# Second attention: where POOL's operations stand, the outputs' division in two parts, two DVE sums in steps of their own

## The chip, the core and the metric

The kernel runs on one core of a Trainium2 chip. The metric is device time in microseconds (us), lower is better. The engines are named as the profile names them: PE is the matrix engine and PEld its weight loads, DVE the vector engine, ACT the scalar engine, POOL the general engine, SP the engine whose queue issues most of the DMAs. A wait belongs to the engine that waits; each engine runs its own instructions in a fixed order, and semaphores order them against the other engines.

## The reference

The input has 16 batches of 512 tokens with 128 features. Two layers follow each other. The first adds a four-fold stack of a state-space block, 16-head attention and a feed-forward block to a feed-forward with ternary weights. It ends before the stage that is changed. The second adds a local attention and a mixture of eight experts. The local attention, cut to what is computed:

```python
q = (x @ Wq) ... ; kv = (x @ Wkv) ...             # 16 heads of 64
q = rotary(q) * SCALE; kv = rotary(kv)
lkv = look_around(kv in windows of 128)           # the window before and its own
lkv = layernorm(lkv, ln_local_g, ln_local_b)      # over the 64 of a head
pkv = softmax(gkv @ Wproj, over each 16 tokens)   # a summary of each segment
gkv = layernorm(sum of gkv * pkv, ln_global_g, ln_global_b)
sim = [q . gkv (32 segments, masked), q . lkv (masked)]
attn = softmax(sim); out = (attn @ [gkv, lkv]) @ Wout + bout
```

The mixture sends each token to one expert (a softmax over eight scores, the largest taken, a rank within the expert, a limit on its places), computes two matmuls with a relu between, weights the result and adds it back at the token's row.

## The kernel before

The second attention works on **units**: 64 tiles of 128 tokens (`u`; four of them, `t` = 0 to 3, are the 512 tokens of a batch). A unit has four **groups** of four heads. Nothing reorders instructions afterwards: each engine runs them in the order in which the program below emits them.

**The main loop.** For group `i` it calls `scores(i)`, then `weights_by_key(i - 1, two)` and `values(i - 2, two)` for `two` = 0 and 1, and after each of these `work(1)`. A group therefore has six calls of `work`. `work` walks a list of generators, the *streams*, and lets each that is due run to its next `yield`. `yield -n` makes a stream due again n calls later; `yield n` does the same and also ends that call of `work`; `yield 0` leaves it due at the next call. If a unit's `front` is not finished when its scores are to begin, the loop calls `work` until it is.

**The streams.** `front(u)` makes the unit's queries and keys and is begun two units ahead. `back(u)` finishes a unit's output and is inserted first in the list when its last scores are done. `routing` computes the expert of each token, scatters the tokens' rows to the experts' places in HBM (`xe_d`, one indirect DMA from POOL's queue for each 128 tokens), and then runs 16 expert halves (`expert_half`). `results` gathers each tile's expert output (`gy`, an indirect DMA from POOL's queue, three buffers), loads the attention's result (`res`) and adds the two on DVE; it begins when the experts are done and can then take one tile after another until it has caught up with the tiles stored.

**One front, with the profile's names.** `xu` is loaded. Two matmuls `m_kv` give keys; DVE multiplies them with cosines (`by_cos`, L1192) and ACT copies them (`raw`, L1193). POOL multiplies `raw` with sines (L1196) and forms `kv` in two halves (L1199, L1200). Four times four matmuls `m_q` and four DVE products `q` (L1210) follow, and POOL adds them in pairs to `qt` (L1218). Then the layer norm over a head: DVE's sum `hm` (L1221) and difference `hd` (L1223), POOL's product `by_w` (L1227), ACT's square `hq` (L1229), DVE's sum `hv` (L1232), ACT's two steps and POOL's five for the root `hr` (L1236 to L1242), and DVE's sum `pl` of `by_w` (L1244). `pl` is transposed on PE (`m_plt`), DVE makes `n` (L1253), `smx` and `se`, and ACT the exponential. After `ss` POOL divides `se` (L1264). Eight transposes `m_nt` of `n` are copied by ACT to the keys `lkt` (L1272); POOL makes the values `lk` in two operations, a product (L1281) and a sum (L1309). `se` goes through `m_pwp` to the segment sums `m_gp`, whose norm (`gm`, `gd`, `gr`, with POOL's L1307 and L1308) gives the segments' values `gv` (L1313, L1314). These go to HBM and come back in four small transfers to `gvb` (L1333), and through `m_gkt` to the keys.

**Scores and values.** `s` is four matmuls; DVE adds the mask and takes the maximum (the pair `pr` and `am`, L1360); ACT takes the exponential and its sum (L1361) and copies the segments' part (`pg`). PE transposes the weights (`gp`, `pp_0`, `pp_1`, L1376 and L1383); DVE and ACT copy them (`gt`, `pt`). `values` adds the products in `o`, which ACT copies to `ot` (L1414), half a unit at a time. The scores are 288 wide, in the first unit of a batch 160.

**One back.** DVE's reciprocal of the sums (L1421), its transpose `m_rd`, a copy to HBM and two broadcasting loads `rb`; POOL multiplies `ot` with `rb` (L1440); nine matmuls `m_po`, DVE's `ro` (L1447) and a store to `r_d`.

**Buffers.** PSUM has five banks for `s`, `gp` and `pp` in turn, two for all that begins with `m_`, and one for `o`. A matmul that takes a bank waits for the reader of what was in it. Most of `front`'s large SBUF tiles have one buffer.

Of the kernel before, what the change touches and what calls it, by code (L numbers as in the profile page):

```python
# [14 lines left out]
ALU = mybir.AluOpType  # L15
# [54 lines left out]
def tile_kernel(  # L70
# [16 lines left out]
    nc = tc.nc  # L87
# [38 lines left out]
    with (  # L126
# [46 lines left out]
        def misc(name):  # L173
            return ps_m.tile([P, S], F32, name=f"m_{name}", tag="m")

        def mm(out, lhsT, rhs, first=True, last=True):
            nc.tensor.matmul(out, lhsT=lhsT, rhs=rhs, start=first, stop=last)  # L177
# [725 lines left out]
        while done_t[0] < n_cycles or ready or streams or due or deferred:  # L903
# [20 lines left out]
            if ready and ready[0][0] <= tick[0]:  # L924
                at, k, i = ready.pop(0)
# [3 lines left out]
            if do_t and done_t[0] % 4 == 3:  # L929
                k, t = divmod(done_t[0], 8)  # L930
# [14 lines left out]
    with (  # L945
# [12 lines left out]
        def const(name):  # L958
            at, n = CONST[name]
            return cst[:, at : at + n]  # L960
# [12 lines left out]
        def row(i):  # L973
            return rows_sb[:, i * DH1 : (i + 1) * DH1]
# [8 lines left out]
        heads = [P, H1, DH1]  # L983
# [155 lines left out]
        def results():  # L1139
# [3 lines left out]
            for t in range(NT):  # L1143
# [12 lines left out]
                nc.vector.scalar_tensor_tensor(res, gy, pk[:, t : t + 1], res, ALU.mult, ALU.add)  # L1156
                nc.sync.dma_start(out[t * P : (t + 1) * P, :], res)

        class Unit:
            pass  # L1160

# [5 lines left out]
        def front(u):  # L1167

            U = units[u] = Unit()
# [13 lines left out]
            def halves(v):  # L1183
                return v.rearrange("p h (a d) -> p h a d", a=2)

            raw = wk.tile(heads, F32, name=f"raw_{u}", tag="raw", bufs=1)
# [6 lines left out]
                nc.scalar.copy(raw[:, 8 * c : 8 * c + 8], psh)  # L1193
                yield 1
            sink = const("sink")[:, t * 32 : (t + 1) * 32].unsqueeze(1).unsqueeze(1).broadcast_to(pair)
            nc.gpsimd.tensor_tensor(halves(raw), halves(raw), sink, ALU.mult)  # L1196
            kv = wk.tile(heads, F32, name=f"kv_{u}", tag="kv", bufs=2)
            k, c_, s_ = halves(kv), halves(by_cos), halves(raw)
            nc.gpsimd.tensor_tensor(k[:, :, 0, :], c_[:, :, 0, :], s_[:, :, 1, :], ALU.subtract)  # L1199
            nc.gpsimd.tensor_tensor(k[:, :, 1, :], c_[:, :, 1, :], s_[:, :, 0, :], ALU.add)  # L1200
            U.qt = wk.tile([P, NHP, P], F32, name=f"qt_{u}", tag="qt", bufs=3)
            for c in range(2):
                parts = []
                for a, name in enumerate(("cosq", "sinq")):
                    ps = misc(f"q_{u}_{c}_{a}")
                    for i in range(4):
                        at = (4 * c + i) * P
                        mm(ps[:, i * P : (i + 1) * P], wq_sb[:, a, at : at + P], x)
                    q = wk.tile([P, 4, P], F32, name=f"q_{u}_{c}_{a}", tag=f"q{a}", bufs=2)
                    nc.vector.tensor_tensor(  # L1210
                        q,
                        ps.rearrange("p (i t) -> p i t", t=P),
                        const(name)[:, t * P : (t + 1) * P].unsqueeze(1).broadcast_to([P, 4, P]),
                        ALU.mult,
                    )
                    parts.append(q)
                    yield 1
                nc.gpsimd.tensor_tensor(U.qt[:, 4 * c : 4 * c + 4, :], parts[0], parts[1], ALU.add)  # L1218
            yield -1
            mean = wk.tile([P, H1], F32, name=f"hm_{u}", tag="hm")  # L1220
# [7 lines left out]
            sq = wk.tile(heads, F32, name=f"hq_{u}", tag="hq", bufs=1)  # L1228
            nc.scalar.activation(sq, d, AF.Square, scale=DH1**-0.5)  # L1229
            yield -2  # L1230
            var = wk.tile([P, H1], F32, name=f"hv_{u}", tag="hv")
            nc.vector.tensor_reduce(var, sq, AX.X, ALU.add)  # L1232
            rstd = wk.tile([P, H1], F32, name=f"hr_{u}", tag="hr")
# [1 line left out]

            nc.scalar.activation(rstd, var, AF.Ln, bias=eps1[:, 0:1])  # L1236
            nc.scalar.activation(rstd, rstd, AF.Exp, scale=-0.5)
            nc.gpsimd.tensor_scalar(hw, var, EPS1, None, ALU.add)
            nc.gpsimd.tensor_tensor(hw, hw, rstd, ALU.mult)
            nc.gpsimd.tensor_tensor(hw, hw, rstd, ALU.mult)  # L1240
# [1 line left out]
            nc.gpsimd.tensor_tensor(rstd, rstd, hw, ALU.mult)  # L1242
            pl = wk.tile([P, H1], F32, name=f"pl_{u}", tag="pl")
            nc.vector.tensor_reduce(pl, by_w, AX.X, ALU.add)  # L1244
            yield -4

            n_seg = P // SEG
            shape = [H1, n_seg, SEG]
# [7 lines left out]
            se = wk.tile(shape, F32, name=f"se_{u}", tag="se")  # L1256
# [4 lines left out]
            ss = wk.tile([H1, n_seg], F32, name=f"ss_{u}", tag="ss")  # L1261
            nc.vector.tensor_reduce(ss, se, AX.X, ALU.add)
            nc.vector.reciprocal(ss, ss)
            nc.gpsimd.tensor_tensor(se, se, ss.unsqueeze(2).broadcast_to(shape), ALU.mult)  # L1264
            U.lk = lks[u % 4]
            for c in range(2):
                ps = misc(f"nt_{u}_{c}")
                n2 = n.rearrange("p h d -> p (h d)")
                for i in range(4):
                    at = (4 * c + i) * P  # L1270
                    nc.tensor.transpose(ps[:, i * P : (i + 1) * P], n2[:, at : at + P], ident)  # L1271
                nc.scalar.activation(  # L1272
                    lkts[b % 2][:, 4 * c : 4 * c + 4, t * KW : t * KW + P],
                    ps.rearrange("p (i t) -> p i t", t=P),
                    AF.Identity,
                    scale=g_col,
                    bias=b_col,
                )
                yield 1
            lk = U.lk  # L1280
            nc.gpsimd.tensor_tensor(lk, n, row(1).unsqueeze(1).broadcast_to(heads), ALU.mult)  # L1281
            ps = misc(f"pwp_{u}")
# [5 lines left out]
                ps[:, 0:H1].rearrange("p (g j) -> p g j", j=4).unsqueeze(3).broadcast_to([P, 4, 4, 32]),  # L1288
                ALU.mult,
            )  # L1290
            yield 2

            gp = misc(f"gp_{u}")
# [12 lines left out]
            nc.vector.tensor_reduce(gr, gq, AX.X, ALU.add)  # L1306
            nc.gpsimd.tensor_scalar(gr, gr, EPS1, None, ALU.add)  # L1307
            nc.gpsimd.tensor_tensor(gr, gr, neg_half[:, 0:1], ALU.pow)  # L1308
            nc.gpsimd.tensor_tensor(lk, lk, row(2).unsqueeze(1).broadcast_to(heads), ALU.add)  # L1309
            yield -1  # L1310
            gv = wk.tile([P, 2, DH1], F32, name=f"gv_{u}", tag="gv")
            nc.scalar.activation(gd, gd, AF.Identity, scale=gr)
# [104 lines left out]
        def back(u):  # L1417

            U = units[u]
            b, t = divmod(u, TB)  # L1420
            nc.vector.reciprocal(U.sum, U.sum)  # L1421
            yield -2
            ps = misc(f"rd_{u}")
            nc.tensor.transpose(ps[0:H1, 0:P], U.sum, ident)
            rd = wk.tile([H1, P], F32, name=f"rd_{u}", tag="rd", bufs=2)
            nc.vector.tensor_copy(rd, ps[0:H1, 0:P])
            yield 2
            nc.sync.dma_start(rd_d[u % 2], rd)
            x1 = wk.tile([P, P], F32, name=f"x1u_{u}", tag="x1u", bufs=2)
            nc.sync.dma_start(x1, x1_d[b][:, t * P : (t + 1) * P])  # L1430
            yield -3
            rb = wk.tile([P, NHP, P], F32, name=f"rb_{u}", tag="rb", bufs=1)
            for a in range(2):
                src = rd_d[u % 2].rearrange("(i a) q -> a i q", a=2)[a]
                nc.sync.dma_start(rb[64 * a : 64 * a + 64], src.unsqueeze(0).broadcast_to([64, NHP, P]))
            while not U.done:
                yield 0
            yield -1
            units.pop(u)
            nc.gpsimd.tensor_tensor(U.ot, U.ot, rb, ALU.mult)  # L1440
            yield -4
            po = misc(f"po_{u}")
            for i in range(NHP):
                mm(po[:, 0:D], U.ot[:, i, :], wout_sb[:, i, :], i == 0, False)
            mm(po[:, 0:D], x1, ident, False, True)
            res = wk.tile([P, D], F32, name=f"ro_{u}", tag="ro", bufs=2)
            nc.vector.tensor_tensor(res, po[:, 0:D], bout_row, ALU.add)  # L1447
            yield 2
            nc.sync.dma_start(r_d[u * P : (u + 1) * P, :], res)
            stored[0] = u + 1  # L1450
            yield -1

        streams = []
        tick = [0]

        def work(n):

            for st in list(streams):
                if st[1] <= tick[0]:
                    wait = next(st[0], None)  # L1460
                    if wait is None:
                        streams.remove(st)
                    elif wait:
                        st[1] = tick[0] + abs(wait)
                        n -= wait > 0
                        if n <= 0:
                            break
            tick[0] += 1

        NU = NT  # L1470
        begun = [0]

        def begin():

            u = begun[0]
            k = sum(1 for st in streams if st[0].__name__ in ("front", "back"))
            streams.insert(k, [front(u), tick[0]])
            begun[0] += 1
# [8 lines left out]
        for i in range(NG1 + 2):  # L1487
            if i % 4 == 0 and begun[0] < NU:
                begin()
            if i < NG1:  # L1490
                while unfinished(i // 4):
                    work(1)
                scores(i)
                work(1)
            for two in range(2):
                if 0 <= i - 1 < NG1:
                    weights_by_key(i - 1, two)
                    work(1)
                if i >= 2:
                    values(i - 2, two)  # L1500
                    work(1)
            work(1)
# [108 lines left out]
```

## Time and profile before

| | |
|---|---|
| median of 3 runs (lowest, highest) | 7816.0 us (7815.46, 7818.84) |
| the profiled execution | 7809.57 us |
| its span | 7807.8 us |
| PE busy | 7008.5 us, 90% |
| DVE busy | 4784.4 us, 61% |
| ACT busy | 4616.8 us, 59% |
| POOL busy | 3012.7 us, 39% |
| second attention | from about 5650 us to the end |

The page gives each engine's busy time over the whole span, and the first layer is almost three quarters of it. For the changed stage the trace is therefore read in stretches: its answer by windows gives the busy time of each engine between two moments, the granted clock of PE and the traffic. A unit is cut from one reciprocal (L1421) to the next. The answer on waits says which engine waited for which, in total, how many times and at most. The timeline gives single instructions, with the start, the duration in us, and in brackets the engine's idle time before one and what ended it.

### The profile page before, as it was taken

What the parts mean: (1) busy time and instruction counts of PE and PEld (TensorE: products, weight loads), DVE (VectorE), ACT (ScalarE), POOL (GpSimd) and SP (SyncE); (2) the same over time, 40 slices, a digit from 0 to 9 for tenths busy, and PEclk for the clock granted to TensorE, in tenths of its full rate; (3) what the DMA queues carried; (4) which work ended last, traced back from release to release, by engine and by line L of the source; (5) the groups of instructions that cost most, each with busy time, mean ns of one, the idle gap of its engine ahead of it and who ended that gap; (6) DMA issues with size and microseconds to landing.
All of it is one profiled execution on the core that took longest, in us unless ns stands there. A gap on an engine that the chain in (4) does not pass through costs nothing. (4 is left out here: it accounts for less than half of the span.)

```text
span 7807.8 us, 107882 instructions
## 1 busy us (share of the span) xinstructions
PE 7008.5 (90%) x38168; PEld 3232.4 (41%) x38168; DVE 4784.4 (61%) x9622; ACT 4616.8 (59%) x9357; POOL 3012.7 (39%) x3763
## 2 busy tenths in 40 slices
PE   6898999999999999999999999999678999888988
PEld 2233333333333333333333333333356666656666
DVE  4565666566666666566666666666366555666665
ACT  3565655666555666666666566656355666556666
POOL 3333332232223233222221222222268655667775
PEclk7899999999999999999999999999789999989999
DMA  2222222212222221122212222222211111111111
GB/s 70 78 83 65 75 70 66 84 64 69 68 71 69 70 66 64 65 64 71 69 61 65 66 74 80 77 77 91 78 33 50 49 42 49 40 46 32 34 35 36
DMA packets 394204, 491.18 MB, mean 63 GB/s; under 512 B 82240, under 2 KB 277952, under 8 KB 392512
## 3 DMA queue, kind: packets, MB, share of 16 engines
q1 hardware_dynamic: 389568, 475.89, 19.5%
q0 software_dynamic: 4096, 8.40, 0.4%
q8 instruction: 302, 4.95, 0.3%
q14 instruction: 238, 1.95, 0.1%
HBM read 348.35 MB, written 132.64 MB: 62 GB/s over the span
## 5 line engine op out<-in xcount | busy, mean ns | idle before, releaser
L921 DVE TENSOR_REDUCE nm<-n 128x1 f32<-128x512 f32 x4096 | 2588.3, 683 | 1459.5 <-PE n L177 1458.0
L923 ACT ACTIVATE pt<-t 128x512 f32<-128x512 f32 x4096 | 2215.3, 595 | 1871.7 <-PE t L177 1847.2
L177 PE MATMUL n<-kt,qt 72*128 72x512 bf16 x4096 | 1319.0, 388 | 200.5 <-DVE nm L921 158.8
L177 PE MATMUL t<-qt,kt 75*128 75x512 bf16 x4096 | 1351.7, 389 | 105.8 <-ACT pt L923 56.5
L177 PE MATMUL o<-pt,vt 128*32 128x512 f32 x8192 | 1131.8, 676 | 0.0
L177 PEld LDWEIGHTS <-qt 72*128 72x128 bf16 x4096 | 354.1, 98 | 1025.5 <-issue 881.3
L177 PEld LDWEIGHTS <-kt 75*128 75x128 bf16 x4096 | 399.2, 99 | 849.2 <-issue 518.3
L1361 ACT ACTIVATE pr<-pr,am 128x288 f32<-128x288 f32 (+1 forms) x1024 | 507.9, 498 | 211.5 <-DVE am L1360 210.6
L873 POOL CAST nmp<-nm 128x16 bf16<-128x16 f32 x256 | 49.9, 195 | 1451.7 <-DVE nm L921 1451.7
L177 PEld LDWEIGHTS o<-pt,vt 128*32 128x32 f32 x8192 | 231.9, 118 | 661.4 <-issue 527.1
L467 POOL TENSOR_TENSOR qk<-qk,parts 128x512 f32<-128x512 f32 x128 | 147.8, 1155 | 770.1 <-ACT parts L280 745.3
L1360 DVE CUSTOM_DVE_ANT_0 pr<-s,cst 128x288 f32<-128x288 f32 (+1 forms) x1024 | 373.0, 420 | 48.4 <-PE s L1004 47.6
L1383 PE MATMUL pp<-ident,pr 128*128 128x128 f32 x1792 | 311.9, 294 | 93.2 <-DVE am L1360 92.2
L1004 PE MATMUL o<-pt,lk 128*64 128x128 f32 x3584 | 328.5, 301 | 0.0
L1385 ACT COPY pt<-pp 128x512 f32<-128x512 f32 (+1 forms) x512 | 264.8, 526 | 97.0 <-PE pp L1383 95.4
L1210 DVE TENSOR_TENSOR q<-m_q,cst 128x512 f32<-128x512 f32 x256 | 177.1, 692 | 220.7 <-PE m_q L1004 220.7
L1004 PE MATMUL s<-lkt,qt 64*128 64x288 f32 (+1 forms) x2048 | 303.3, 414 | 0.4 <-ACT lkt L1327 0.4
L177 PE MATMUL m_in<-x,w 128*128 128x512 f32 x512 | 277.4, 627 | 17.1 <-POOL x L330 8.9
L1383 PEld LDWEIGHTS pp<-ident,pr 128*128 128x128 f32 x1792 | 215.0, 148 | 161.5 <-DVE am L1360 128.1
L1004 PE MATMUL m_q<-xu,wq_sb 128*128 128x128 f32 x2048 | 279.6, 280 | 1.3 <-ACT raw L1193 0.3
L177 PE MATMUL m_f<-n,w 128*128 128x512 f32 x512 | 272.5, 615 | 2.9 <-POOL n L330 2.6
L1004 PEld LDWEIGHTS m_q<-xu,wq_sb 128*128 128x128 f32 x2048 | 250.7, 193 | 19.3 <-ACT raw L1193 15.2
(336 smaller groups left out, 11103.9 us busy)
## 6 DMA issues: line engine op xcount, KB each, us to landing
qt<-q_d SPq DMA_DIRECT2D x768, 96.0 KB
kt<-k_d SPq DMA_DIRECT2D x256, 288.0 KB
rb_n<-rstd_d SPq DMA_DIRECT2D x64, 512.0 KB
rb<-rd SPq DMA_DIRECT2D x128, 256.0 KB
q_d<-parts SPq DMA_DIRECT2D x64, 384.0 KB
k_d<-parts SPq DMA_DIRECT2D x64, 384.0 KB
o_d<-og SPq DMA_DIRECT2D x512, 36.0 KB
oa<-o_d SPq DMA_DIRECT2D x64, 256.0 KB
```

Of the source, the lines that this page charges most:

```text
L177: nc.tensor.matmul(out, lhsT=lhsT, rhs=rhs, start=first, stop=last)
L467: nc.gpsimd.tensor_tensor(x, x, parts[:, 0], ALU.subtract)
L873: nc.gpsimd.tensor_copy(parts[:, 0], nm)
L921: nc.vector.tensor_reduce(dst, n, AX.X, ALU.max, negate=True)
L923: nc.scalar.activation(dst, n, AF.Exp)
L1004: nc.tensor.matmul(out, lhsT=lhsT, rhs=rhs, start=first, stop=last)
L1210: nc.vector.tensor_tensor(q, ps.rearrange("p (i t) -> p i t", t=P), const(name)[:, t * P : (t + 1) * P].unsqueeze(1).broadcast_to([P, 4, P ...
L1360: nc.vector.tensor_tensor_reduce(pr[:, j, 0:n], s[:, 0:n], mask(t), -1.0, BIG, ALU.add, ALU.min, nmax)
L1361: nc.scalar.activation(pr[:, j, 0:n], pr[:, j, 0:n], AF.Exp, bias=nmax, scale=-1.0, accum_out=U.sum[:, 4 * g + j : 4 * g + j + 1])
L1383: nc.tensor.transpose(pp[:, a, c, :], G.pr[:, 2 * two + a, at : at + P], ident)
L1385: nc.scalar.copy(pt[:, :, 0:n, :], pp[:, :, 0:n, :])
```

## The change

A generator `quiet` yields 0 as long as `phase` is 4 or 5. `phase` counts the calls of `work` since the last scores. In `front`, the steps with `hv` and with `pl` begin only after `quiet`, and `hv` with ACT's two steps is parted by a yield of its own from POOL's five and `pl`; the yield after these is one shorter. POOL's three operations on `raw` and `kv` are emitted after the first `q`, the division of `se` after the first copy to `lkt`, the sum of `lk` one step earlier, ahead of `gr`. In `back`, `ot` is multiplied in two halves: the first after the loads of `rb`, the second where the whole stood.

```diff
+        def quiet():
+            while phase[0] in (4, 5):
+                yield 0
...
-            nc.gpsimd.tensor_tensor(halves(raw), halves(raw), sink, ALU.mult)
...
-            nc.gpsimd.tensor_tensor(k[:, :, 0, :], c_[:, :, 0, :], s_[:, :, 1, :], ALU.subtract)
-            nc.gpsimd.tensor_tensor(k[:, :, 1, :], c_[:, :, 1, :], s_[:, :, 0, :], ALU.add)
...
                     parts.append(q)
                     yield 1
+                    if c == a == 0:
+                        nc.gpsimd.tensor_tensor(halves(raw), halves(raw), sink, ALU.mult)
+                        nc.gpsimd.tensor_tensor(k[:, :, 0, :], c_[:, :, 0, :], s_[:, :, 1, :], ALU.subtract)
+                        nc.gpsimd.tensor_tensor(k[:, :, 1, :], c_[:, :, 1, :], s_[:, :, 0, :], ALU.add)
...
             yield -2
+            yield from quiet()
             var = wk.tile([P, H1], F32, name=f"hv_{u}", tag="hv")
             nc.vector.tensor_reduce(var, sq, AX.X, ALU.add)
...
             nc.scalar.activation(rstd, rstd, AF.Exp, scale=-0.5)
+            yield -1
+            yield from quiet()
             nc.gpsimd.tensor_scalar(hw, var, EPS1, None, ALU.add)
...
             nc.vector.tensor_reduce(pl, by_w, AX.X, ALU.add)
-            yield -4
+            yield -3
...
-            nc.gpsimd.tensor_tensor(se, se, ss.unsqueeze(2).broadcast_to(shape), ALU.mult)
...
                 yield 1
+                if c == 0:
+                    nc.gpsimd.tensor_tensor(se, se, ss.unsqueeze(2).broadcast_to(shape), ALU.mult)
...
+            nc.gpsimd.tensor_tensor(lk, lk, row(2).unsqueeze(1).broadcast_to(heads), ALU.add)
             yield 2
...
             nc.gpsimd.tensor_tensor(gr, gr, neg_half[:, 0:1], ALU.pow)
-            nc.gpsimd.tensor_tensor(lk, lk, row(2).unsqueeze(1).broadcast_to(heads), ALU.add)
...
+            yield -3
+            nc.gpsimd.tensor_tensor(U.ot[:, 0:4, :], U.ot[:, 0:4, :], rb[:, 0:4, :], ALU.mult)
             while not U.done:
                 yield 0
             yield -1
             units.pop(u)
-            nc.gpsimd.tensor_tensor(U.ot, U.ot, rb, ALU.mult)
+            nc.gpsimd.tensor_tensor(U.ot[:, 4:8, :], U.ot[:, 4:8, :], rb[:, 4:8, :], ALU.mult)
...
+        phase = [0]
...
             tick[0] += 1
+            phase[0] += 1
...
                 scores(i)
+                phase[0] = 0
                 work(1)
```

## The prediction

> **What bounds it now.** I read the waits of the whole stage first, then the busy times unit by unit (cut at the reciprocal L1421, once per unit), then single rows. The second attention runs from about 5650 us to the end; only there does the change act. Units 2 to 60 span 5778.6 to 7742.2, 1963.6 us, in four stages: **A**, units 2 to 10, routing's scatters (33.2 us a unit, 11 is mixed at 30.5); **B**, 12 to 27, one expert half each (36.4); **C**, 28 to 36, four gathers each (36.5); **D**, 37 to 60, one gather each (30.1). One unit of each:
>
> ```profile
> core 0: us, PE busy (x) PEld busy (x) DVE busy (x) ACT busy (x) POOL busy (x), PEclk, DMA share, GB/s
> 5911.36:5944.47 33.11, 28.61 (x243) 21.43 (x241) 20.73 (x60) 20.38 (x59) 27.78 (x27) 0.91 0.19 54
> 6289.56:6326.37 36.81, 35.02 (x294) 25.67 (x290) 21.01 (x60) 22.91 (x63) 20.64 (x19) 1.00 0.19 52
> 6873.96:6912.27 38.31, 30.32 (x246) 22.59 (x246) 22.83 (x64) 20.37 (x58) 23.79 (x23) 0.91 0.16 43
> 7139.89:7170.40 30.51, 27.12 (x248) 20.24 (x246) 20.49 (x60) 20.16 (x58) 21.73 (x20) 1.00 0.13 34
> ```
>
> After the first column come the length and each engine's busy time. PE is the fullest everywhere, so only its gaps can be won: 33.11 - 28.61 in A, 1.8 us in B, 8.0 in C, 3.4 in D. What ended them (engine, line, waited for, total, times, longest):
>
> ```profile
> PE pp L1383 <- DVE am L1360: 75.9, 43, 2.9
> PE m_po L1004 <- POOL ot L1440: 57.7, 52, 2.9
> PE o L1004 <- DMA gvb<-gv: 32.5, 7, 5.2
> PE m_nt L1271 <- DVE se L1257: 25.9, 21, 1.4
> ```
>
> These are what the change aims at. The first is a buffer: pp_0 takes the bank of s_0, the fifth before it, and cannot start until am_0 has read that. The reader should see DVE late for it, behind two long sums:
>
> ```profile
> 7164.57 1.21 DVE L1232 TENSOR_REDUCE hv<-hq 128x16 f32<-128x1024 f32 x1
> 7166.56 1.22 DVE L1244 TENSOR_REDUCE pl<-by_w 128x16 f32<-128x1024 f32 x1 [0.78 <-POOL by_w L1227]
> 7167.70 0.45 DVE L1360 CUSTOM_DVE_ANT_0 pr<-s,cst 128x288 f32<-128x288 f32 x1
> 7168.21 0.66 PE L1383 MATMUL pp<-ident,pr 128*128 128x128 f32 x4 [1.64 <-DVE am L1360]
> ```
>
> **The parts.** I followed the built instruction order on each engine. *raw, kv and the softmax weights' product moved in the text*: they stand where they stood in POOL's order, so 0. *lk's sum moved up*: its 2.36 us leave the way of gd and gv and lie in POOL's idle before gr (3.08 us at 7148.56): 0 of itself. *pl and hv*: they now follow the four am of the last group; m_plt and with it n, smx, se move behind the reciprocal, ahead of the next unit's first am. *ot in halves*: two operations of 1.27 (the row of kv, same 128x512) for one of 2.37, 0.17 more POOL time. *What moves with it*: m_gp goes behind m_kv_0, so gm, gd, gr come a group later; two of the four gvb transfers go behind r_d in SP's queue; scatters, gathers and expert steps land elsewhere.
>
> **D, a full unit, from the reciprocal at 0.** m_rd 0.30 (6765.62 to 6765.92), rd at 0.61. res is ahead of rd and waits for its gather, which POOL now issues after by_w (ends 27.5, that is -2.3): landing 2.7 after its start, so res at 0.5 and n at 0.99. n, smx, se take 1.07 + 0.30 + 0.21: am_0 at 2.57, pp_0 0.51 later, where PE could have been at 1.83: a gap of 1.25. On ACT am_0 + 0.50 + 2.22 gives pg 5.29, then pt_0 and lkt (0.20 + 0.48 + 0.77): m_pwp, which needs lkt's bank, at 6.85. Then 0.16 + 1.01 + 1.03 + 0.59: group 1 at 9.6 (T1). By gr, ACT's raw and pt_0, gd reaches POOL at T1 + 5.2 and raw, queued behind gv, starts at T1 + 6.06; before it was 4.39 (7153.51 - 7149.12). Then 2.43 + 3 x 1.22 + 1.27: the second half of ot at T1 + 13.4, against 12.86 whole before. PE is there at 12.2, does the four matmuls of the first half (0.95), waits 0.3, and ends po and two o at T1 + 15.55 (T3). am_0 0.78, four am 1.52, hv 1.15, gt 0.20, pl 1.14: reciprocal at T3 + 4.79; m_rd waits for it about 0.9. Sum 9.6 + 15.55 + 4.79 = 29.95, against 30.5. With 160-wide scores 28.15, the mixed unit 29.8: mean **29.5** against 30.1. The two old stalls go, but gaps of 1.25, 0.5, 0.3 and 0.9 take their place: the chain of latencies through DVE, ACT and POOL is nearly as long as before.
>
> **B.** PE's work is 35.0. New order: xep before gp, hp_0 before group 2's scores, hp_1 and hp_2 before po, yp in the last group. Gaps by the same sums: pp_0 0.5; m_nt_1 needs xep's bank, whose copy stands in ACT behind four exponentials: 1.0; hp_2 behind the lkt copies 0.45; po needs hp_1's bank, whose relu now stands behind hq, which waits for hd: 0.75. Sum 2.7. In every second unit xe's load stands behind ye_d and both weights in SP's queue; two 256 KB transfers took 2.6 us (6414.1 to 6416.7), so four end 4.4 after the reciprocal, and xep, 2.3 late, costs 0.6. Full units 37.7 and 38.2 against 36.8; over the four kinds **37.4** against 36.4. The cover was good before: xep had 15 us.
>
> **A.** Three scatters of 1.2 us now stand between by_w and the five hw operations in POOL, where one stood. n waits for hr, so the hw chain (1.5 us) ends 33.1 after n: by_w 27.95, scatters to 31.6, hw. The unit is POOL's own chain, 33.2, and PE idles 4.5 us at pp_0 until am_0. About 0.9 for the clock: **34.1**. And the order holds 6 scatters a unit for 7: stage A lasts 11 units, to unit 12.
>
> **C.** Five gathers a unit instead of four: 7.4 units instead of 9. By the semaphores (three gy buffers) the gather issued behind by_w serves the res just before group 3's am. The old order waits little there:
>
> ```profile
> 6724.24 1.03 POOL L1147 DMA_INDIRECT gy<-ye_d,slot  x1 [0.15 <-issue]
> 6726.93 0.35 DVE L1156 SCALAR_TENSOR_TENSOR res<-gy,pk,res 128x128 f32<-128x128 f32 x1 [1.58 <-DMA gy<-ye_d,slot]
> ```
>
> 2.7 us from issue to use. New: qt ends 25.2, a gather, by_w to 28.9, the gather at 29.0, res at 31.75, am_0 at 32.0 instead of 25.9. PE stands 6 us. The 5 us waits on gvb go. Unit 36.0 + 1.7 for the clock = **37.7** against 36.5.
>
> [...] Clock. The row: after 1.9 us idle the eight po took 3.57 us instead of 2.05.
>
> ```profile
> 7101.69 3.57 PE L1004 MATMUL m_po<-wout_sb,ot 128*128 128x128 f32 x16 [1.89 <-POOL ot L1440]
> ```
>
> [...] The rows:
>
> ```profile
> 7159.61 2.38 POOL L1440 TENSOR_TENSOR ot<-ot,rb 128x1024 f32<-128x1024 f32 x1
> 7161.93 2.28 POOL L1218 TENSOR_TENSOR qt<-q,q 128x512 f32<-128x512 f32 x1
> 7161.73 1.35 DVE L1223 SCALAR_TENSOR_TENSOR hd<-hm,kv 128x1024 f32<-128x1024 f32 x1
> ```
>
> [...] qt here takes 1.0 more than the 1.29 of its twin at 7158.38. [...]
>
> **The sum.** 11 x 34.1 + 16 x 37.4 + 7 x 37.7 + 32 (unit 36) + 24 x 29.5 = 1977 against 1964: +13. My rows make 26.75 us of PE work in a D unit where 27.12 are measured; half of that on the path, 0.18 x 58, adds 10. The last units, where ot's last half is 1.1 shorter, give back 2. Start: 0, at most 5 either way. So +21 or 22 on the profiled 7809.6 (span 7807.8): 7831; the median shown, 7816.0, lies 6.4 above that execution: **7838**.
>
> **Rivals.** *Faster: indirect transfers hide.* If POOL runs ahead so that res finds its gather landed and hr is done before the scatters, C loses 7.4 x 7 and A 11 x 1.5 beyond: about -68 against the forecast, 7770. For it: POOL is busy only 39%; against: its order is fixed and by_w ends late. It decides from a gather issued 3 us before its res. *A draw:* D's gain of 14 and C's fewer units pay for B: within 0.2% (15.6 us, about what a measurement can tell), 7816. [...] That the change does nothing is excluded by the order.
>
> **Chances.** Forecast's own case 0.42 (7825 to 7862), faster rival 0.22, draw 0.20, heavier 0.16. Sharing the edges: faster 0.24, same 0.22, slower 0.54. The range reaches to the rivals' bounds: 7770 to 7895.
>
> **What would show it.** PE's waits: pp on am in group 3 gone in B and D, new ones of 1 us at pp_0 of group 0 and at m_rd; m_nt on xeT and po on he in B; res on gy with 4 to 6 us a unit in C; n on hr of 3 to 4 us in A; raw on POOL 1.7 later after group 1's scores. I am wrong if C's units fall below 32, or B's stay at 36.4, or D's go below 29.

## The result, and the profile after

| | before | after |
|---|---|---|
| median (lowest, highest) | 7816.0 us (7813.78, 7835.29; 7 runs) | 7839.7 us (7834.21, 7858.72; 7 runs) |
| ratio after to before, 95% interval | | 1.0036 [1.0024, 1.0048] |
| profiled execution | 7809.57 us | 7847.59 us |
| PE busy | 7008.5 us | 6983.7 us |

The changed kernel is slower by 0.36%, 24 us. PE has 25 us less busy time and the kernel still takes longer: what was lost are gaps. The profiled execution lies 8 us above its own median, that of before 6 us below, so the two traces stand 38 us apart where the medians stand 24 apart. From unit 2 to 60 PE's busy time went from 1744.0 to 1720.1 us, and the rest, its gaps, from 219.7 to 288.4. Cut at the reciprocal (L1421 before, L1431 after), by stage:

| stage | before | forecast | after |
|---|---|---|---|
| from the start to unit 2 | 5778.6 | 0 | 5775.6 |
| A, scatters, us a unit | 33.2 | 34.1 | 35.2 (11 units) |
| B, experts | 36.4 | 37.4 | 38.6 (16) |
| C, gathers | 36.5 | 37.7, then 32 | 36.5 (7), then 30.0 |
| D, one gather | 30.1 | 29.5 | 29.95 (24) |
| units 2 to 60 together | 1963.6 | 1977 + 10 | 2008.5 |
| from unit 61 to the end | 65.6 | -2 | 61.7 |

The units shown of before have these counterparts in the trace after: one of A, B and C, a full one of D, and the mixed one (160-wide and 288-wide scores) of D ahead of it.

```profile
core 0: us, PE busy (x) PEld busy (x) DVE busy (x) ACT busy (x) POOL busy (x), PEclk, DMA share, GB/s
5876.90:5912.61 35.71, 29.47 (x246) 21.53 (x246) 20.53 (x60) 20.28 (x58) 27.62 (x27) 0.90 0.16 45
6358.04:6396.79 38.75, 34.77 (x292) 25.50 (x291) 21.50 (x62) 23.26 (x63) 20.78 (x20) 1.00 0.13 35
6888.61:6925.81 37.20, 28.76 (x221) 20.34 (x218) 22.67 (x66) 19.37 (x58) 25.88 (x26) 0.87 0.18 49
7305.98:7335.87 29.89, 27.06 (x246) 20.30 (x246) 20.70 (x62) 20.07 (x59) 21.88 (x22) 1.00 0.13 35
7273.64:7305.98 32.34, 28.64 (x226) 20.46 (x226) 21.13 (x62) 19.31 (x59) 22.31 (x24) 0.89 0.13 34
```

Read the length against PE's busy time: the gap in B has grown from 1.8 to 4.0 us at full clock, while the full unit of D has 2.8 for 3.4. The mixed unit has fewer matmuls than the full one and takes longer, at a clock of 0.89. PE's waits from unit 2 to 60, after:

```profile
PE pp L1393 <- DVE am L1370: 105.2, 51, 7.3
PE o L1004 <- DMA gvb<-gv: 37.9, 14, 3.5
PE m_rd L1434 <- DVE sum L1431: 28.4, 33, 1.1
PE m_pwp L1293 <- ACT lkt L1280: 27.2, 42, 1.3
PE m_po L1004 <- ACT he L1128: 21.7, 16, 1.9
PE m_po L1004 <- POOL ot L1452: 20.5, 41, 1.1
PE m_xep L1120 <- DMA xe<-xe_d: 13.2, 7, 2.7
PE m_nt L1279 <- ACT xeT L1122: 10.3, 8, 1.5
PE m_hp L1004 <- ACT lkt L1337: 9.9, 16, 0.8
```

The wait of `m_po` for `ot` has fallen from 57.7 to 20.5, that of `m_nt` for `se` is gone; five kinds are new (`m_pwp` on `lkt`, `m_po` on `he`, `m_xep`, `m_nt` on `xeT`, `m_hp` on `lkt`), `m_rd` waits 28.4 for 5.0, and the wait at `pp` has grown although the two sums no longer stand in front of it.

Two places show how. In stage A, POOL around the end of a unit, DVE, and the transpose on PE that waits behind it:

```profile
5945.09 2.39 POOL L1233 TENSOR_TENSOR by_w<-kv,rows_sb 128x1024 f32<-128x1024 f32 x1
5947.64 1.01 POOL L1091 DMA_INDIRECT xe_d<-xts,slot  x1 [0.17 <-issue]
5950.18 0.96 POOL L1091 DMA_INDIRECT xe_d<-xts,slot  x1 [1.54 <-DMA xe_d<-xts,slot]
5953.15 0.96 POOL L1091 DMA_INDIRECT xe_d<-xts,slot  x1 [2.00 <-DMA xe_d<-xts,slot]
5954.14 0.28 POOL L1247 TENSOR_SCALAR hw<-hv 128x16 f32<-128x16 f32 x1
...
5955.65 1.22 DVE L1262 TENSOR_TENSOR n<-hd,hr 128x1024 f32<-128x1024 f32 x1 [6.11 <-POOL hr L1251]
...
5957.67 1.11 PE L1393 MATMUL pp<-ident,pr 128*128 128x128 f32 x4 [7.34 <-DVE am L1370]
```

A scatter shows 1 us on POOL, but the next two here wait 1.54 and 2.00 us for the one before to land (2.4 us from issue to landing in the median of this trace's 64), and their starts lie 2.5 and 3.0 apart. From the end of `by_w` (5947.48) to `hw` pass 6.7 us. `n` waits 6.11 for `hr`, and `pp_0` 7.34 behind the `am` that follows `n`. This is the longest such wait; `n` waits for `hr` in six of the eleven units, 18.8 us together. In the mixed unit of D, on DVE and then on PE:

```profile
7273.64 0.24 DVE L1431 RECIPROCAL sum<-sum 128x16 f32<-128x16 f32 x1
7274.94 0.35 DVE L1156 SCALAR_TENSOR_TENSOR res<-gy,pk,res 128x128 f32<-128x128 f32 x1 [1.05 <-DMA gy<-ye_d,slot]
...
7275.41 1.20 DVE L1262 TENSOR_TENSOR n<-hd,hr 128x1024 f32<-128x1024 f32 x1
...
7277.56 0.44 PE L1393 MATMUL pp<-ident,pr 128*128 128x128 f32 x2 [1.80 <-DVE am L1370]
```

The addition `res` stands in DVE's queue ahead of `n` and waits 1.05 for its gather; everything behind it, `am` and so `pp_0`, is that much later.

### The profile page after: what moved, and what is told of

Its sections match the earlier page's. It is cut to its first block, busy times and chain, and to the rows that moved or that the text cites. A ratio compares the mean times of both kernels' runs of the same rounds, so it can differ in the third digit from the quotient of the medians.

```text
span 7845.8 us, 107802 instructions
## 1 busy us (share of the span) xinstructions
PE 6983.7 (89%) x38168; PEld 3208.2 (41%) x38168; DVE 4779.2 (61%) x9622; ACT 4618.6 (59%) x9357; POOL 3042.3 (39%) x3827
```

## The experiments

My theory was: the change itself wins a little in a unit, but the steps of the two sums shift what routing, the experts and the results issue to places where it blocks a queue. The rivals: the moved POOL operations or the halves cost it (1); the clock (2 and 3). Each ratio below is to the kernel before, run again beside the kernel in question (its medians lie between 7811 and 7828 us).

**The parts of the change.** First the sums' steps alone on the kernel before (with `quiet` and `phase` as in the change), and everything but them.

```diff
 # sum_steps_only, on the kernel before
...
             yield -2
+            yield from quiet()
             var = wk.tile([P, H1], F32, name=f"hv_{u}", tag="hv")
...
             nc.scalar.activation(rstd, rstd, AF.Exp, scale=-0.5)
+            yield -1
+            yield from quiet()
...
-            yield -4
+            yield -3
```

> The kernel before with only the two long sums in steps of their own (quiet twice, the added yield, the shorter last yield); POOL's operations and the whole ot stay where they were. The order built from it has the scatters (5 to 7 a unit, to unit 12), expert halves (units 13 to 28) and gathers (five a unit) of the whole change. Theory (these steps alone shift the shared streams and cost it): stage B, units 13 to 28, at 38 to 39 us a unit against 36.4 before; total 7840, between 7825 and 7855. Rival 1 (the moved POOL operations or the two halves of ot cost it): B within 0.5 us of before, total 7800 to 7820. Stage D under the theory: m_po waits for the whole ot again, 24 times 1 us, so 0.3 to 0.8 a unit worse than the whole change's 29.95.

8036.9 us, ratio 1.0266 [1.0252, 1.0281]: neither theory foresaw it. Stage B takes 40.9 us a unit, and D 33.8 where the whole change has 29.95. PE's first wait in D, then POOL and PE in one of its units:

```profile
PE m_po L1004 <- POOL ot L1448: 77.4, 24, 3.9
```

```profile
7373.68 0.57 POOL L1316 TENSOR_TENSOR gr<-gr,neg_half 128x1 f32<-128x1 f32 x1
7374.23 2.35 POOL L1317 TENSOR_TENSOR lk<-lk,rows_sb 128x1024 f32<-128x1024 f32 x1
7376.55 0.31 POOL L1321 TENSOR_TENSOR gd<-gd,rows_sb 128x64 f32<-128x64 f32 x1
...
7377.35 2.36 POOL L1201 TENSOR_TENSOR raw<-raw,cst 128x1024 f32<-128x1024 f32 x1
...
7383.46 2.35 POOL L1448 TENSOR_TENSOR ot<-ot,rb 128x1024 f32<-128x1024 f32 x1
...
7385.86 3.78 PE L1004 MATMUL m_po<-wout_sb,ot 128*128 128x128 f32 x16 [3.93 <-POOL ot L1448]
```

The steps bring `gr` a group later; `lk`'s sum (2.35 us) then stands between `gr` and `gd`, `raw` and the whole `ot` queue up behind it, and `m_po` waits 3.9 us and then runs 3.78. So the other parts do not come on top of the sums' steps: together they repair most of what these do. How much of it the moves do and how much the halves, no run shows.

> The changed kernel without the steps of the sums: POOL's moved operations and the halved ot remain, the shared streams stand where they stood before. Theory: m_po's wait for ot (57.7 us in 52 waits before) shrinks to under 20, most of it won, stages A, B and C otherwise as before: total 7770 to 7800. Rival 1: what remains of the change costs, 7830 or more. Rival 2 (the ot wait hides other waits, the chain of latencies takes it all back): 7805 to 7820.

```diff
 # on the changed kernel
-            yield from quiet()
...
-            yield -1
-            yield from quiet()
...
-            yield -3
+            yield -4
```

7772.4 us, ratio 0.993 [0.9916, 0.9943]: faster than both kernels, as the theory had it. B takes 35.25 us a unit, D 29.3, and `m_po` waits for `ot` 0.5 us from unit 2 on.

> The kernel before with ot divided in halves and nothing else. all_but_sum_steps gave 7772 against 7824 for the kernel before; this and pool_only part its gain. Theory: the halves bring it, since the first half lies in POOL's idle before raw and PE can begin m_po with four of its matmuls; m_po's wait for ot (57.7 us in 52 waits before) falls under 15 and the time to 7775 to 7800. Rival (the moved POOL operations, lk's sum ahead of gr above all, bring it): 7805 to 7825.

```diff
+            yield -3
+            nc.gpsimd.tensor_tensor(U.ot[:, 0:4, :], U.ot[:, 0:4, :], rb[:, 0:4, :], ALU.mult)
             while not U.done:
...
-            nc.gpsimd.tensor_tensor(U.ot, U.ot, rb, ALU.mult)
+            nc.gpsimd.tensor_tensor(U.ot[:, 4:8, :], U.ot[:, 4:8, :], rb[:, 4:8, :], ALU.mult)
```

Ratio 0.9957 [0.9942, 0.9971]; `m_po` waits 13.7 us for `ot`. The halves bring most of it.

> The kernel before with POOL's moved operations (raw and kv in the text, the division of se, lk's sum ahead of gr), ot whole, the sums' steps as before. Theory: raw waits for ACT's copy either way, so lk's sum moved up frees POOL time that nothing used: 7810 to 7830, m_po's wait for ot within 15 us of 57.7. Rival (these moves bring the gain of all_but_sum_steps): 7775 to 7795.

The edit is all_but_sum_steps with the whole `ot` back in place:

```diff
-            yield -3
-            nc.gpsimd.tensor_tensor(U.ot[:, 0:4, :], U.ot[:, 0:4, :], rb[:, 0:4, :], ALU.mult)
...
-            nc.gpsimd.tensor_tensor(U.ot[:, 4:8, :], U.ot[:, 4:8, :], rb[:, 4:8, :], ALU.mult)
+            nc.gpsimd.tensor_tensor(U.ot, U.ot, rb, ALU.mult)
```

Ratio 1.0005 [0.9997, 1.0013], the wait for `ot` 55.1 us: POOL's moves alone bring nothing, as expected. (Their trace is 18 us longer than that of before from unit 2 to 60, 1981.5 against 1963.6, though the medians are equal: a difference of that size between two single traces proves nothing by itself.) With the halves they seem to: 0.993 against 0.9957, two intervals that just touch, and `m_po` waits 0.5 us for `ot` instead of 13.7. The reason is an argument and was not tried by itself: `lk`'s sum ahead of `gr` opens the place in which the first half of `ot` then lies.

**The unit by itself.** Three kernels leave the mixture of experts out.

```diff
-        streams += [[other_weights(), tick[0]], [routing(), tick[0] + 60], [results(), tick[0]]]
+        streams += [[other_weights(), tick[0]], [results(), tick[0]]]
```

and `results` neither gathers nor adds.

> The kernel before without routing, scatters, expert halves and gathers: the output is the attention's result alone, the mixture of experts is left out. All units then should look like stage D: 59 units from 2 to 60 at 29.8 to 30.1 us (30.1 in stage D with a gather), total 7600 to 7640. This is the base for its twin.

> The changed kernel without routing, scatters, expert halves and gathers: the mixture of experts is left out. Theory (the change itself wins little, its loss comes from the shared streams): 10 to 35 us below its twin before_alone (59 units by 0.15 to 0.6). Rival 1 (the moved operations themselves cost): 10 us or more above its twin. Rival 3 (the clock falls with the new small gaps, whatever the shared streams do): a granted clock lower than its twin's by 0.02 or more over units 2 to 60 and a time equal or above.

> all_but_sum_steps without routing, scatters, expert halves and gathers; the mixture of experts is left out. Third of a set with before_alone (ratio 0.9744) and change_alone (0.9661). Theory (the sums' steps give a unit by itself nothing): within 0.0015 of change_alone, full units 29.4 against 29.9, 160-wide units 28.0 against 27.5. Rival (they gain by themselves and lose only through the shared streams): 0.9685 or more.

| | ratio to the kernel before | units 2 to 60, alone | the same with the mixture | difference |
|---|---|---|---|---|
| before | 0.9744 [0.9729, 0.9759] | 1780.1 us | 1963.6 | 183.5 |
| all but the sums' steps | 0.9648 [0.9626, 0.9669] | 1722.3 | 1923.2 | 200.9 |
| the whole change | 0.9661 [0.9642, 0.968] | 1730.3 | 2008.5 | 278.2 |

By itself a changed unit is 0.84 us faster than before ((1780.1 - 1730.3) / 59), more than theory or forecast had. Rival 1 falls. Units 2 to 60 in the three traces, in the order of the table:

```profile
5765.49:7545.59 1780.10, 1587.69 (x13789) 1185.92 (x13787) 1179.62 (x3482) 1142.94 (x3423) 1216.54 (x1121) 0.96 0.12 32
5752.26:7474.58 1722.32, 1560.88 (x13805) 1166.65 (x13801) 1173.21 (x3481) 1143.83 (x3422) 1231.29 (x1180) 0.97 0.13 33
5773.31:7503.61 1730.30, 1533.07 (x13794) 1141.68 (x13794) 1186.90 (x3482) 1141.26 (x3423) 1227.56 (x1181) 0.99 0.13 33
```

Rival 3 falls too: the clock is 0.99 for 0.96. More than that, the clock is where the gain lies: with nearly the same matmuls PE is busy 54.6 us less, while its gaps (length less busy time) are 192.4 us before and 197.2 with the whole change. Only the kernel without the sums' steps has smaller gaps, 161.4. Why the clock is higher with the sums' steps, no run shows. In sum these steps add nothing to a unit (1730.3 against 1722.3).

With the mixture beside them they cost 77 us more than without it (278.2 - 200.9; 73 by the ratios). This is the theory's core, and it is shown.

**Stages C and D: the additions.** DVE's wait for the gathers and PE's first wait, after, in units 29 to 36:

```profile
DVE res L1156 <- DMA gy<-ye_d,slot: 42.7, 15, 4.0
```

```profile
PE pp L1393 <- DVE am L1370: 48.4, 17, 5.8
```

```diff
                 nc.sync.dma_start(res, r_d[t * P : (t + 1) * P, :])
-                yield -3
+                yield -8
                 nc.vector.scalar_tensor_tensor(res, gy, pk[:, t : t + 1], res, ALU.mult, ALU.add)
```

> The changed kernel with one number different: results waits 8 calls instead of 3 between its gather and the addition, so no addition stands on DVE before its gather has landed; the order built has two gathers a unit from unit 29 to 56 instead of five to unit 35 and one after. Theory (stage C pays for additions that block DVE ahead of a group's am): DVE's waits on gy (42.7 us in stage C, 8.2 in D) fall under 5, units 29 to 35 go from 36.5 to 31 to 32.5 us, units 37 to 60 stay within 0.6 of 29.95: total 25 to 40 us below the whole change. Rival 1 (each gather costs what it costs, wherever its addition stands): the same total within 8 us. Rival 2 (the clock of the mixed unit falls for its own gaps): mixed units stay at 32.3, as in the whole change; under the theory they fall to 29.5 to 31.

Ratio 0.9972 [0.9962, 0.9983], 50 us below the whole change, more than expected. DVE no longer waits for `gy` from unit 29 on; units 29 to 35 take 29.8 us in the mean ((6982.58 - 6773.72) / 7). The edit also spreads the gathers: two a unit from unit 29 to 57, where the whole change has five a unit to unit 35 and one after unit 36. Whether the later addition or the spread wins, no run parts; PE's waits behind DVE speak for the addition. Of the 50 us 46 are won in units 29 to 36 and 4 in D. The same mixed unit as above, in this kernel, and PE's wait at its `pp_0`; then a later mixed unit of this kernel:

```profile
7221.38:7251.18 29.80, 26.04 (x226) 18.96 (x226) 21.11 (x62) 19.13 (x58) 23.02 (x23) 1.00 0.16 41
```

```profile
7224.35 0.44 PE L1393 MATMUL pp<-ident,pr 128*128 128x128 f32 x2 [0.85 <-DVE am L1370]
```

```profile
7340.49:7370.70 30.21, 28.61 (x226) 20.73 (x226) 21.12 (x63) 19.23 (x58) 22.89 (x22) 0.89 0.16 41
```

A mixed unit of D takes 30.05 us in the mean of six, where the whole change has 31.8. Rival 1 falls: as many gathers cost 50 us less. Rival 2 falls too, since no mixed unit takes 32.3 us any more. But the lower clock does not follow the wait: three of these six units ran at 0.89 without it, and in the whole change one of the six ran at 1.00 with it:

```profile
7634.02:7664.55 30.53, 25.81 (x226) 18.97 (x226) 21.04 (x62) 19.30 (x59) 22.29 (x24) 1.00 0.13 36
```

```profile
7638.04 0.44 PE L1393 MATMUL pp<-ident,pr 128*128 128x128 f32 x2 [1.92 <-DVE am L1370]
```

So the wait of 1.05 us for a gather and the clock are to be counted apart. Between units at a clock of 1.00 the whole change is 0.7 us longer than this kernel (30.53 against 29.80), between units at 0.89 about 2.1 (32.3 against 30.2).

**Stage B: the place of the expert half.** The half waits longer between the load of `xe` and `m_xep`.

```diff
-            yield -3
+            yield -9
             ps = misc(f"xep_{nm}")
```

> The changed kernel with one number different: an expert half waits 9 calls instead of 3 after the load of xe before its transposes m_xep. In the order built m_xep stands behind the last m_q as hp_0 did, hp_0 and hp_1 ahead of m_po (hp_1 and hp_2 before), and there is one half a unit as before. Theory (stage B pays for waits that its place in the unit makes): m_xep's wait for xe (13.2 us), m_nt's for xeT (10.3) vanish and m_po's for he (21.7) falls by half or more; stage B from 38.6 to between 36.3 and 37.4 us a unit; total 20 to 35 us below the whole change. Rival (the half's work on PE and ACT sets it wherever it stands, or the clock does): 38 or more, total within 10 us.

Ratio 1.0012 [1.0, 1.0023], 19 us below the whole change by the ratios and just short of the 20 expected. PE's waits in stage B:

```profile
PE m_po L1004 <- ACT he L1128: 20.0, 16, 1.9
PE pp L1393 <- DVE am L1370: 18.0, 16, 4.1
PE m_pwp L1293 <- ACT lkt L1280: 13.2, 15, 1.3
PE m_hp L1004 <- ACT lkt L1337: 9.9, 16, 0.8
```

The waits for `xe` and `xeT` are gone as foreseen. `m_po` waits as before, against my expectation: it needs one relu less, but ACT still does that one behind `hq`. And `pp` and `m_pwp` wait more. A unit takes 37.7, not 36.3 to 37.4, against 35.25 without the sums' steps.

**Stage A: the loads of the rows.** In stage A after, SP waited 211.9 us at the loads of `xts`, and PE 37.9 for `gvb`, whose transfers stand behind them. That is more than the 22.8 us, in six units, that PE waited at `pp` there.

```profile
SPq L1089 <- DMA xe_d<-xts,slot: 211.9, 60, 11.8
```

```diff
-            for t in range(NT + 3):
+            for t in range(NT + 2):
...
-                    xts[t] = wk.tile([P, D], F32, name=f"xts_{t}", tag="xts", bufs=4)
+                    xts[t] = wk.tile([P, D], F32, name=f"xts_{t}", tag="xts", bufs=5)
...
-                if t >= 3:
+                if t >= 2:
...
```

> The changed kernel with the rows that routing scatters (xts) in five buffers instead of four and scattered two steps after their load instead of three: each load then waits for a scatter three steps back instead of one. Theory (stage A pays on SP: a load of xts that waits for its buffer holds up gv and gvb behind it in SP's queue): SP's wait at the loads of xts falls from 211.9 us to under 100, PE's wait for gvb from 37.9 us to under 10, units 2 to 12 from 35.2 to between 33.0 and 34.3 us a unit; total 10 to 25 us below the whole change. Rival (what the prediction said: hr stands behind the scatters in POOL's queue, and n waits for it): A stays at 34.8 or more, n's wait for hr (18.8 us) stays or grows.

Ratio 1.0045 [1.0027, 1.0064]: no gain. SP's wait fell to 72.5 and PE's for `gvb` to none, as the theory said, yet a unit of A takes 36.4 us. DVE's and PE's first waits in A:

```profile
DVE n L1262 <- POOL hr L1251: 58.6, 10, 6.0
```

```profile
PE pp L1393 <- DVE am L1370: 68.1, 11, 7.1
```

`n` waits for `hr` in ten units instead of six, 5.9 us each, and `pp` behind it: the rival, the prediction's cause. Both held the stage; where SP was late, the wait for `hr` lay beside it.

**Together.** The first kernel has these three edits on the changed kernel; the second has those of `results` and of `xts` on all_but_sum_steps.

> The changed kernel with the three edits together: results waits 8 calls, an expert half 9, xts in five buffers and two steps ahead. Theory: the three places are separate and their gains add: 50 (measured), 19 (measured) and 10 to 25, so a ratio to the kernel before of 0.991 to 0.994. Rival (a gain in one place is given back in another): 0.996 or more.

Ratio 0.997 [0.9958, 0.9983], at the rival's end. In the trace the edits add: units 2 to 60 take 1948.2 us against 2008.5, -60.3, where the single ones give -50.0, -17.9 and +5.9. That is most of the 77 us that the sums' steps cost beside the mixture. My sum had counted the third as a gain; with its measured ratio the four figures give 0.9957, still 10 us below the measured ratio.

> all_but_sum_steps with results waiting 8 calls and xts in five buffers and two steps ahead; the expert half's wait is as before, since its place was good. Theory (the sums' steps are no gain, the halves and POOL's moves are): gathers at two a unit give 35 to 50 us on the 0.993 of all_but_sum_steps, ratio 0.986 to 0.989, and 20 us or more below change_three_fixes. Rival (the sums' steps gain once the shared streams are out of their way): change_three_fixes is equal or lower.

Ratio 0.9986 [0.9977, 0.9995]: slower than without the two edits (0.993), where a gain of 35 to 50 us was expected. PE's first wait from unit 29 on, then SP's longest:

```profile
PE o L1004 <- DMA gvb<-gv: 74.0, 19, 4.7
```

```profile
SPq L1157 <- DVE gt L1385: 240.7, 25, 10.1
...
SPq L1157 <- DVE ss L1268: 122.6, 18, 7.0
```

L1157 is the store of `out`, which waits for the addition. With 8 calls it falls between `gv` and the four `gvb` loads of SP's queue, and its addition stands behind `gt` on DVE; `gvb` comes late and PE stops at `o`. In change_res_late the same store stands ahead of `gv`, and PE waits 3.5 us for `gvb` in all. Units 2 to 27 take 891.9 us against 895.8 without the edits, so the loss (40.2 us in the trace) is all behind them, where only the wait of `results` differs (it was not run by itself on this kernel). Whether that wait wins 50 us or loses 40 hangs, by these rows, on a place in one queue. The fastest version tried is all_but_sum_steps.

## Why the prediction came out

The time, 7838 for 7839.7, was right, and so was the sign. It was partly luck: the sum was +21 or 22 on the profiled execution, which measured +38; the medians came nearer because the profiled execution after happens to lie 8 us above its median, that of before 6 below. Units 2 to 60 took 21 us more than the forecast's 1987: A 12, B 19 and D 11 more, C with unit 36 10 less, and the 10 added for PE's work had covered part of it.

- **D's chain.** A full unit at 29.95: measured 29.89, and 29.9 alone. The `pp_0` gap (1.25, measured 1.2), `m_rd` (0.9 and 0.94) and `ot` (0.3 and 0.5) were right. The mixed unit at 29.8 was wrong: 32.2 to 32.6 in four of six. Left out were the wait of `res` for its gather, taken to land in time ("res at 0.5"), and the lower clock: the one unit of the six that ran at 1.00 took 30.5. Alone that unit takes 29.5 or 31.0.
- **PE's busy time.** "Only its gaps can be won" was wrong. In D the gaps grew from 77.9 to 81.6 us, and its gain of 4 us is PE's busy time (644.9 and 637.3); for a unit by itself the rows of the three kernels without the mixture show the same.
- **B.** Every wait named came, two larger: `m_po` on `he` 1.36 a unit for 0.75 (21.7 / 16), and `m_xep` 1.24 (13.2 + 4.5 + 2.2, over 16) for 0.3. These two make 1.55 of the miss of 1.2; `m_nt` came to 0.64 for 1.0.
- **A.** The cause, `hr` behind scatters, was right but held only six of the eleven units; change_xts_early laid it bare. The mis-sized term is "three scatters of 1.2": of the 33 that waited for another in this stage, 30 started 2.5 to 3.5 us after it, and three, with the root's operations between, 3.7 to 4.2. The trace of before had that in a row I did not read: 14 scatters waited 21.0 us, 1.5 each, for the one ahead. What I did not see was SP, held at the loads of `xts` ahead of `gvb`, PE's longest wait of the stage in total.
- **C.** The mechanism was right: `res` on `gy`, 42.7 us in 8 units, and `pp` 48.4. It was sized a little too high, 37.7 for 36.5. And the faster rival's price was near: "C loses 7.4 x 7" is 52, and making the gathers land in time, and spreading them, was worth 46 in C. A bare gap is not the whole of it: of the 46, 29 are gaps and 18 PE's busy time, 226.3 us for 208.6 (the clock was 0.90 there after, and 0.99 in change_res_late from unit 29 to 60).
- **POOL's moves, "0 of itself".** True on the kernel before (1.0005). In the changed order it is open: without them and the halves D takes 33.8 for 29.95, and no run parts the two there. I priced the parts one by one against the old order, and so did not see that the sums' steps alone would cost 2.7%.
- **`hd` beside POOL.** The sum has no term for it, and `ot` lost nothing: its second half took 1.25 to 1.28 us in all 24 units of D, where the forecast had 1.27. `hd` overlaps it and the `qt` behind it, and took 1.85 to 2.26 us, 2.03 in the median (before 1.33 to 2.29, and 1.42); that `qt` took 2.25 to 2.27, its twin 1.26 to 1.29. Why they are longer there, no run shows.
- **The clock.** No run shows the sum's terms for it, 0.9 us a unit in A and 1.7 in C. What was measured is a granted clock of 0.91 before and 0.89 after in A, 0.88 and 0.90 in C, and in PE's busy time for each matmul 0.122 and 0.121 us in A, 0.127 and 0.120 in C. Nor did the length of an idle time foretell it. In the trace before, `m_po` took 3.57 us at 7101.69 (a clock of 0.54 over the row) and 2.05 us at 7222.21 (1.00) after the same wait of 1.89:

```profile
7222.21 2.05 PE L1004 MATMUL m_po<-wout_sb,ot 128*128 128x128 f32 x16 [1.89 <-POOL ot L1440]
```

In the trace after, the mixed unit shown ran at 0.89 with no wait above 1.80, and a mixed unit with a wait of 1.92 ran at 1.00. In change_res_late, where PE's longest wait in D was 1.5, three mixed units ran at 0.89. What decides, no run here shows.

## What to carry to other kernels

Where several streams share hand-ordered queues, a yield added to one moves them all: run the change once without the neighbours (here -50 us from unit 2 to 60) and once with them (+45), and it is plain which of the two is being measured. Before a stall is removed, look for the one that lies beside it. And read the waits between two instructions of the same kind: the row of a scatter showed 1 us here, its spacing was 2.5 us and more.

## What was unexpected in the hardware

The scatters to `xe_d` that wait for each other start 2.5 to 4.2 us apart in stage A after, though 56 of the 64 show 0.96 to 1.11 us on POOL. And the granted clock did not follow the length of the idle times: waits of 1.80 and 1.92 us in the same place of two units went with 0.89 and 1.00, PE's busy time for the same 226 matmuls being 28.6 and 25.8 us. The start of the changed stage differs between profiled executions: unit 2 begins anywhere from 5752 to 5796 us over these kernels, so stages are compared from there and the totals by medians.
